# An AdaLN, recurrence and mixture-of-experts block: order of batch 3's steps, expert order from two batches, batch 0 in halves, the condition by a product

## The chip, the cores and the metric

One Trainium2 chip, one core. The time is device microseconds of the whole program; the figure of the kernel before is the median of three runs.

## The reference, cut to what matters

Four batches of 256 tokens with 256 channels, all in float32. `side` gives both keys and values.

```python
def wkv(r, k, v, w, u, time_emb):               # two directions of a decayed sum over the tokens
    tf = sigmoid(sum(time_emb))                 # one number a batch, from the condition
    decay = exp(-exp(w)) * (0.5 + 0.5 * tf)
    ek = exp(min(k, 30)); ekv = ek * v
    nf, df = forward scans;  nb, db = reverse scans
    num = nf + nb - ekv + exp(u + k) * v;  den = df + db - ek + exp(u + k)
    return sigmoid(r) * num / max(den, 1e-8) * (0.8 + 0.2 * tf)

def recurrence(x, W_in, b_in, W_gate, b_gate, lam):
    alpha = exp(-8 * softplus(lam) * sigmoid(x @ W_gate + b_gate))
    h = scan(alpha, sqrt(1 - alpha**2 + 1e-6) * sigmoid(x @ W_in + b_in) * x)
    return h

def ffn(x, w_router, wg, wu, wd, sg, su, sd):   # 8 experts, top 2, and 2 shared ones; 640 hidden
    scores = sigmoid(x @ w_router.T)            # the two best, weights made to sum to 1
    return routed experts (SwiGLU) + shared experts (SwiGLU)

x = x + recurrence(wkv(x, side, side, w1, u1, cond), ...)
x = x + ffn(wkv(x, side, side, w2, u2, cond), ...)
```

The router weighs each token's logits; an expert computes only the tokens that chose it.

## The kernel before

Activations are channel-major: a tile holds 128 channels by 2 x 256 columns (two halves of the channels, the tokens of one batch). A 512-column operation covers a batch.

**Start.** `par` (small vectors), `cond` (spread to all 128 partitions by the DMA), batch 0's `x` and `wio` are issued on ACT's queue, the `side` tiles, batch 1, `wr` and the two shared experts (`shared`) on SP's. PE runs warm-up products of `ident` meanwhile (L355 plain, L358 in four tiled quarters; WARM sets how many).

**A batch's front** (`front(b)`). `half_tanh` (xc), `exps` (L447 to L461), `sums` (reverse scans L479, forward scans L547 on DVE; for batch 0 the parts are added on PE by products with `ident`, L509; elsewhere on DVE, L534 and L536, or by an adding DMA, L523), `most` (L563), `quotient` (Ln and Exp on ACT, L579 and L580; L581, L582, L584 on DVE), `gates` (L601, products with `wio` L612, tanh L620, square root L649), `recurrence` (L656, scans L661, sum into x L667, tanh L668, product L670, giving `xt`). `fill` (L518) puts products of `ident` on PE where it would stand idle during batch 0. Then `token_rows`: transposes of `xt` (L748), router products (L753), `scores` (L759), copies into token rows (L762).

**Routing.** `route` turns scores into ranks, `chosen`, `upto` (a running count by tile of 128 tokens) and `comb` (L778 to L805). It runs once for batches 0 to 2 and once for batch 3. `places` counts with two products (`counted`: L892 with `ones` and `upto`, L893 with `before` and `chosen`) and gives each token its row in an expert's region; `scatter` (L1110, POOL) sends token rows there, and eight `blank` DMAs (L1123, ACT's queue) put empty rows behind each region's last. In the call for batches 0 to 2, a third product (L896) counts what was chosen so far, and `line_up` ranks the experts by it, busiest first, into `order_eid`; `first_weights` then loads the weights of the first four experts (`quad`, three DMAs of 640 KB each, L1202). `divide` (L1033 to L1107), after batch 3, deals the remaining tiles of 128 tokens to slots; their weights go to a `ring`.

**Shared experts** (`shared_units(b)`). Two experts of five units each: four products of 256 columns into one of four PSUM banks (L836), SiLU (L842, ACT), product (L844, DVE), and two down products a unit (L821), up to three units later. Base rows: transposes of x (L859), copies (L863), sum with the shared result (L865), output DMA (L879, SP).

**Experts.** The list of slots and groups runs after everything above: transposes of gathered rows (L1189), gate and up products (L1212), SiLU and product (L1217, L1218), down products (L1225), weighting (L1232), scatter-add into the output (L1241, POOL). LAST dummy products (L1501) on PE end it; a branch (L1503) for more tiles follows, which isn't taken with these inputs.

**What sets the order.** All before the experts is recorded as steps in the class `Plan`: engine, length, what it reads and writes, a rank (smaller goes first), and `late`, the time after a step's end until another engine may take its result for done. `Plan.run` goes through time: at each point the engine whose next step can start earliest takes the ready step of lowest rank. NUDGE adds to the ranks of single steps. The steps are then emitted in that order, and every engine executes its own list strictly in it. The lengths and `late` are only the planner's figures; on the chip each instruction waits for what it truly needs.

Of the kernel before, what the change touches and what calls it, by code (L numbers as in the profile page):

```python
# [8 lines left out]
F32 = mybir.dt.float32  # L9
# [9 lines left out]
P = 128  # L19
# [39 lines left out]
ACTS, DEPTH, WARM, KEEP, FILL, LAST = 6, 3, 12, 6, 4, 7  # L59
# [27 lines left out]
    ("divide", "dve", "blank_row"): -6,  # L87
    ("exps", 0, "act", "ek"): -5,
    ("exps", 0, "act", "own"): -6,
    ("exps", 0, "dve", "own"): 1,  # L90
    ("exps", 1, "dve", "ek"): -6,
    ("exps", 2, "dve", "ek"): 14,
    ("exps", 2, "dve", "own"): 9,
    ("exps", 3, "dve", "ek"): 6,
    ("exps", 3, "dve", "own"): 5,
    ("factors", "dve", "decay1"): 14,
    ("gates", 1, "act", "gate"): 5,
    ("gates", 1, "act", "xb"): -5,
    ("gates", 2, "pe", "one"): 6,
    ("gates", 3, "act", "gate"): 5,  # L100
    ("gates", 3, "act", "xb"): -5,
    ("gates", 3, "dve", "xc"): 10,
    ("line_up", "dve", "order_at"): 11,
    ("loads", "act", "xr"): 2,
    ("most", 3, 2, "act", "fwd"): 5,
    ("places", 0, "pe", "one"): 9,
    ("quotient", 1, 2, "act", "inv"): 16,
    ("quotient", 1, 2, "dve", "fwd"): 20,
    ("recurrence", 0, "dve", "xt"): 12,
    ("recurrence", 3, "dve", "xb"): 7,  # L110
    ("route", 0, "dve", "comb"): 1,
    ("route", 0, "dve", "upto"): 5,
    ("route", 3, "dve", "comb"): -5,
    ("rows", 0, "dve", "scores"): 24,
    ("rows", 2, "dve", "scores"): 23,
    ("rows", 2, "pe", "one"): 5,
    ("rows", 3, "pe", "one"): 7,
    ("shared", 0, "act", "act"): 37,
    ("shared", 0, "pe", "acc"): -4,
    ("shared", 0, "pe", "bank"): -6,  # L120
    ("shared", 1, "pe", "bank"): -1,
    ("shared", 1, "pe", "one"): -10,
    ("shared", 2, "pe", "acc"): 1,
    ("sums", 0, 1, "dve", "fwd"): 1,
    ("sums", 0, 1, "dve", "rev"): 1,
    ("sums", 0, 2, "pe", "bank"): -5,
    ("sums", 1, 1, "dve", "rev"): -13,
    ("sums", 1, 2, "dve", "fwd"): 4,
    ("sums", 1, 2, "dve", "own"): 3,
    ("sums", 1, 2, "dve", "rev"): 5,  # L130
    ("sums", 2, 1, "dve", "fwd"): 1,
    ("sums", 2, 2, "dve", "fwd"): -3,
    ("sums", 2, 2, "dve", "rev"): -3,
    ("sums", 3, 2, "dve", "fwd"): -15,
    ("sums", 3, 2, "dve", "own"): 5,
    ("sums", 3, 2, "dve", "rev"): 4,
# [102 lines left out]
def adaln_attn_ffn(ctx: ExitStack, tc, xT, sideT, cond, par, wio, wr, wall, out):  # L239
# [17 lines left out]
    cond_sb = fixed("cond_sb", B, TD)  # L257
    nc.scalar.dma_start(cond_sb, cond.partition_broadcast(P))
# [20 lines left out]
    load_batch(0, nc.scalar)  # L279
    nc.scalar.dma_start(wio_sb, wio)  # L280
# [7 lines left out]
    nc.scalar.preload_act_table_set(EXP)  # L288
    ident = fixed("ident", P)
# [64 lines left out]
    for k in range(WARM):  # L354
        nc.tensor.matmul(banks[k % BANKS][:, 0, 0:P], ident, ident, start=True, stop=True)  # L355
    for k in range(2 * WARM):
        q = 32 * (k % 4)
        nc.tensor.matmul(  # L358
            banks[k // 8][q : q + 32].rearrange("p g t -> p (g t)")[:, 0:P], ident[:, 0:32], ident,
            start=True, stop=True, tile_position=(0, q),  # L360
        )
    acc = [psum.tile([P, 2 * C], F32, name=f"acc{j}")[:, 0:C] for j in range(TB)]
    ones_ps = [psum.tile([P, 2, T], F32, name=f"one{k}") for k in range(2)]
# [4 lines left out]
    def halves(name, *rest):  # L368
        return [(name, *rest, h) for h in range(2)]

# [9 lines left out]
    def pe(cols, emit, reads=(), writes=(), rank=0, **kw):  # L380
        return step("pe", 1.625 * cols + 16, emit, reads, writes, rank, late=205, **kw)
# [8 lines left out]
    given(("side", 0), 4400)  # L390
    given("cond", 4600)
    given(("x", 0), 6000)
    given("wio", 8000)
    given(("side", 1), 8500)
    given(("x", 1), 9000)
# [4 lines left out]
    given(("x", 2), 23000)  # L400

    def factors():

        plan.part = ("factors",)
        dve(250, lambda: nc.vector.tensor_reduce(tf, cond_sb, AX.X, ALU.add), ["cond"], ["tf"], 11)
# [109 lines left out]
    def fill(after, times, writes=()):  # L515

        for k in range(times):
            pe(P, lambda: nc.tensor.matmul(acc[1][:, 0:P], ident, ident, start=True, stop=True), (), writes, 99, after=[after])  # L518
# [46 lines left out]
    def quotient(b, n):  # L565
# [9 lines left out]
        if (b, n) in BY_PE:  # L575
# [7 lines left out]
        dve(  # L583
            512, lambda: nc.vector.scalar_tensor_tensor(f[:, NC:, :], num, out_tf[:, b : b + 1], y, ALU.mult, ALU.mult),  # L584
            nkeys + yk + ["out_tf"], ns, r,
        )
        return f[:, NC:, :], ns

    def half_tanh(b):
        plan.part = ("half_tanh", b)  # L590
        act(
            512, lambda: nc.scalar.activation(xc, xs[b], AF.Tanh, scale=0.5), [("x", b % 3)], ["xc"], 10 * b + 19,
# [3 lines left out]
    def gates(b, q, qkeys):  # L596
# [4 lines left out]
        dve(512, lambda: nc.vector.scalar_tensor_tensor(xc, xc, 1.0, q, ALU.add, ALU.mult), ["xc"] + qkeys, ["xc"], r)  # L601
        for which, dst, name in ((1, gate, "gate"), (0, xb, "xb")):
# [6 lines left out]
            for m, (key, pio) in enumerate(to):  # L609
                for k in range(NC):  # L610
# [5 lines left out]
                        ["xc", "wio"], [key], 0,  # L616
# [9 lines left out]
        dve(512, lambda: nc.vector.scalar_tensor_tensor(xb, xb, 1.0, xc, ALU.add, ALU.mult), xbs + ["xc"], xbs, r + 1)  # L626
# [22 lines left out]
        act(512, lambda: nc.scalar.activation(gate, gate, AF.Sqrt, bias=eps, scale=-1.0), gs, gs, r, tables=(SQRT,), hold=(name, True))  # L649
# [959 lines left out]
```

## Time and profile before

| | |
|---|---|
| median of three runs | 297.46 us (297.28 to 297.73) |
| the profiled execution | 296.47 us |
| its span | 294.8 us |
| mean granted clock of PE | 0.985 of full speed |
| PE, DVE, ACT, POOL busy | 95%, 59%, 43%, 21% of the span |
| bytes moved by DMA | 51.68 MB |
| first scan on DVE | 8.23 us |
| token rows of batches 0, 1, 2, 3 begin on PE | 32.07, 63.90, 94.76, 124.55 us |
| first transpose of the expert stretch | 162.59 us |

A row of the timeline is: start in us, length in us, engine, line, operation, tile written <- tiles read, shapes, count; in brackets the idle time before and what ended it. Rows of the same line in a row are drawn together. A float32 product of 256 columns shows as two records, one of 128 columns also as two. A row of windows gives, per engine, busy time and number of instructions, then PE's granted clock, the share of the DMA engines in use and GB/s. "SPq" and "ACTq" are DMA issues on that queue.

### The profile page before, as it was taken

What the parts mean: (1) busy time and instruction counts of PE and PEld (TensorE: products, weight loads), DVE (VectorE), ACT (ScalarE), POOL (GpSimd) and SP (SyncE); (2) the same over time, 40 slices, a digit from 0 to 9 for tenths busy, and PEclk for the clock granted to TensorE, in tenths of its full rate; (3) what the DMA queues carried; (4) which work ended last, traced back from release to release, by engine and by line L of the source; (5) the groups of instructions that cost most, each with busy time, mean ns of one, the idle gap of its engine ahead of it and who ended that gap; (6) DMA issues with size and microseconds to landing.
All of it is one profiled execution on the core that took longest, in us unless ns stands there. A gap on an engine that the chain in (4) does not pass through costs nothing. (4 is left out here: it accounts for less than half of the span.)

```text
span 294.8 us, 5521 instructions
## 1 busy us (share of the span) xinstructions
PE 281.2 (95%) x1945; PEld 243.5 (83%) x1945; DVE 173.6 (59%) x493; ACT 127.6 (43%) x253; POOL 61.4 (21%) x102
## 2 busy tenths in 40 slices
PE   7999999999999999995999999999999999999990
PEld 7889888888888888874888768999868997698990
DVE  3999999999999987944532443223443225334220
ACT  5768879967395869750111221122121112112200
POOL 8820000000100011771300002210142222242421
PEclk9999999999999999997899999999999999999998
DMA  4962030002300040279988999999847798322211
GB/s 141 425 275 91 3 71 0 2 0 71 71 2 1 0 86 23 95 263 419 299 280 279 395 413 409 374 395 394 294 88 255 229 382 302 57 27 31 23 22 22
DMA packets 19665, 51.68 MB, mean 175 GB/s; under 512 B 2736, under 2 KB 11824, under 8 KB 19376
## 3 DMA queue, kind: packets, MB, share of 16 engines
q1 hardware_dynamic: 13216, 42.46, 37.9%
q0 software_dynamic: 3792, 6.06, 11.0%
q10 hardware_dynamic: 2624, 2.74, 2.8%
q8 instruction: 17, 0.28, 0.4%
q14 instruction: 16, 0.13, 0.1%
HBM read 54.43 MB, written 7.05 MB: 209 GB/s over the span
## 5 line engine op out<-in xcount | busy, mean ns | idle before, releaser
L836 PE MATMUL bank<-xt,shared 128*128 128x256 f32 x320 | 75.0, 389 | 0.0
L836 PEld LDWEIGHTS bank<-xt,shared 128*128 128x128 f32 x320 | 62.2, 196 | 8.6
L1212 PE MATMUL bank<-side,late 128*128 128x128 f32 x400 | 47.7, 276 | 0.0
L1212 PEld LDWEIGHTS bank<-side,late 128*128 128x128 f32 x400 | 46.3, 192 | 1.3 <-issue 1.0
L1218 DVE TENSOR_TENSOR act<-bank,act 128x256 f32<-128x256 f32 (+1 forms) x42 | 15.9, 380 | 47.1 <-ACT act L1217 43.5
L1241 POOL DMA_INDIRECT outT<-ys,to x14 | 21.6, 1546 | 101.4 <-DMA xr<-rows 37.4
L1217 ACT ACTIVATE act<-bank 128x256 f32<-128x256 f32 (+1 forms) x42 | 14.6, 349 | 54.1 <-PE bank L1212 50.2
L821 PE MATMUL acc<-shared,act 128*128 128x256 f32 x160 | 37.9, 381 | 0.1
L821 PEld LDWEIGHTS acc<-shared,act 128*128 128x128 f32 x160 | 30.1, 190 | 4.5 <-DVE act L844 0.5
L221 ACT ACT_TABLE_LOAD x24 | 30.8, 1283 | 0.4
L842 ACT ACTIVATE act<-bank 128x256 f32<-128x256 f32 x40 | 13.8, 383 | 31.4 <-PE bank L836 16.7
L844 DVE TENSOR_TENSOR act<-bank,act 128x256 f32<-128x256 f32 x40 | 15.6, 417 | 15.1 <-ACT act L842 14.1
L1225 PE MATMUL acc<-late,act 128*128 128x256 f32 x100 | 23.4, 381 | 0.0
L1232 DVE TENSOR_SCALAR ys<-acc,w 128x256 f32<-128x256 f32 (+1 forms) x18 | 8.5, 472 | 23.2 <-PE acc L1225 16.3
L523 POOL DMA_DIRECT2D late<-late x3 | 2.9, 952 | 87.2 <-DVE late L536 37.7
L547 DVE TENSOR_TENSOR_SCAN late<-decay,late 128x256 f32<-128x256 f32 x32 | 20.8, 674 | 0.0
L1225 PEld LDWEIGHTS acc<-late,act 128*128 128x128 f32 x100 | 18.2, 190 | 3.1 <-issue 0.5
L1110 POOL DMA_INDIRECT rows<-xtok,where x16 | 16.6, 1036 | 20.0 <-DVE at L919 10.0
L1192 ACT COPY side<-one 128x256 f32<-128x256 f32 x17 | 6.2, 373 | 33.5 <-PE one L1189 31.1
L479 DVE TENSOR_TENSOR_SCAN late<-late,decay 128x255 f32<-128x255 f32 x32 | 20.2, 669 | 0.0
L1212 PEld LDWEIGHTS bank<-side,quad 128*128 128x128 f32 x120 | 13.9, 192 | 1.1 <-issue 0.5
L1212 PE MATMUL bank<-side,quad 128*128 128x128 f32 x120 | 14.5, 277 | 0.2 <-ACT side L1192 0.2
(256 smaller groups left out, 396.4 us busy)
## 6 DMA issues: line engine op xcount, KB each, us to landing
late<-in_wall SPq DMA_DIRECT2D x33, 640.0 KB
quad<-in_wall SPq DMA_DIRECT2D x27, 640.0 KB
shared<-in_wall SPq DMA_DIRECT2D x9, 640.0 KB
shared<-in_wall SPq DMA_DIRECT2D x2, 1920.0 KB
late<-late POOLq DMA_DIRECT2D x3, 512.0 KB
xr<-rows SPq DMA_DIRECT2D x10, 136.0 KB
rows<-empty ACTq DMA_DIRECT2D x8, 136.0 KB
side<-in_sideT SPq DMA_DIRECT2D x4, 256.0 KB
```

The lines of the kernel that those rows point to most:

```text
L221: order.append((max(free.get(engine, 0), 0), len(order), lambda t=table: load_table(t)))
L479: 0, lambda h=h, c=c: nc.vector.tensor_tensor_scan(r[:, h, 0 : T - 1][:, ::-1], src[:, h, 1:T][:, ::-1], dec[:, c, b : b + 1].to_broadcast ...
L547: 0, lambda: nc.vector.tensor_tensor_scan(f[:, h, :], dec[:, c, b : b + 1].to_broadcast([P, T]), src[:, h, :], 0.0, ALU.mult, ALU.add),
L821: 256, lambda j=j: nc.tensor.matmul(acc[j], acts[a][:, bass.ts(j, P)], shared[s][:, GU + i * C : GU + (i + 1) * C], start=((s, i) == (0, 0 ...
L836: 256, lambda ps=ps, gu=gu, g=g, c=c, i=i: nc.tensor.matmul(ps[:, g, :], gu[:, g, c, bass.ts(i, P)], xt[k][:, c, :], start=(c == 0), stop= ...
L844: 256, lambda ps=ps, av=av: nc.vector.tensor_tensor(av, ps[:, 1, :], av, ALU.mult),
L1110: i = nc.gpsimd.indirect_dma_start(out=rows[:, :], out_offset=bass.IndirectOffsetOnAxis(ap=where[:, k, t : t + 1].bitcast(U32), axis=0), i ...
L1212: nc.tensor.matmul(ps[:, g, i, :], gu[:, g, k, bass.ts(i0 + i, P)], self.xg[:, k, :], start=(k == 0), stop=(k == NC - 1),)
L1217: nc.scalar.activation(hid[:, 0:n, :], ps[:, 0, 0:n, :], AF.Silu)
L1218: nc.vector.tensor_tensor(hid[:, 0:n, :], ps[:, 1, 0:n, :], hid[:, 0:n, :], ALU.mult)
L1225: nc.tensor.matmul(self.py, self.acts[i], self.weights[:, GU + i * C : GU + (i + 1) * C], start=(i == 0), stop=(i == NI - 1),)
L1241: nc.gpsimd.indirect_dma_start(out=out[:, :], out_offset=bass.IndirectOffsetOnAxis(ap=to.bitcast(U32), axis=0), in_=ys, in_offset=None, bo ...
```

## The change

- **Order of batch 3.** A step on PE may be given its own `late`. The products of the first two units of the first shared expert of batch 3 get 4200 ns instead of 205. With the ranks in NUDGE (a new table throughout) and scatter's `late` of 4000, the emitted order becomes: on DVE all of `route` directly behind batch 3's scores, `places` next, then L844 of unit 2, unit 0 and unit 1; on ACT SiLU of unit 2, unit 0, one blank-row DMA, unit 1, seven blank-row DMAs, then the other units; on PE behind the token rows two products of unit 0, four transposes (L859), two more, four of unit 1, two of unit 2, the counting pair, and the rest.
- **Expert order from batches 0 and 1** (NGUESS). A new `guess()` takes the scores (logits) of the first two batches before `route`, holds them at SAME = 16.7, takes off a thousandth of the expert's number, marks the two largest of each token, counts with four products of `ones`, and calls `line_up`. L896 and the call in `places` fall away. `first_weights` is split: the first two experts' weights are issued on SP after the tanh of batches 1 and 2, the other two after that of batch 3.
- **Batch 0's last steps in halves.** `x`, `xc` and `xt` carry keys by half, and for batch 0 the last step of the first quotient, the first of the gates, the square root, L656, L667, L668 and L670 are emitted as two 256-column operations. Token-row transposes and shared products wait for the half they read.
- **The condition by a product.** `cond` is loaded as one row of 1 KB on SP and spread by a product of a row of ones into PSUM (`cond_all`), which DVE reduces. In the emitted order that product is the first on PE. All first loads but `par` go on SP: side 0, cond, x 0, wio, side 1, x 1, wr, shared.
- WARM 12 to 4 (plain products 2 x 4, tiled 3 x 4, instead of 12 and 24), FILL 4 to 3, LAST 7 to 14. The fill products write a part of PSUM that nothing else uses.

```diff
-ACTS, DEPTH, WARM, KEEP, FILL, LAST = 6, 3, 12, 6, 4, 7
+ACTS, DEPTH, WARM, KEEP, FILL, LAST = 6, 3, 4, 6, 3, 14
+NGUESS = 2
+SAME = 16.7
 NUDGE = {
...
-    cond_sb = fixed("cond_sb", B, TD)
-    nc.scalar.dma_start(cond_sb, cond.partition_broadcast(P))
+    cond_sb = fixed("cond_sb", B * TD)
...
-    load_batch(0, nc.scalar)
-    nc.scalar.dma_start(wio_sb, wio)
+    load_side(0)
+    nc.sync.dma_start(cond_sb[0:1, :], cond.rearrange("b d -> (b d)").unsqueeze(0))
+    load_x(0, nc.sync)
+    nc.sync.dma_start(wio_sb, wio)
...
-    for k in range(WARM):
+    cond_all = ones_ps[1][:, 0, 0 : B * TD]
+    for k in range(2 * WARM):
         nc.tensor.matmul(banks[k % BANKS][:, 0, 0:P], ident, ident, start=True, stop=True)
-    for k in range(2 * WARM):
+        if k == WARM - 1:
+            nc.tensor.matmul(cond_all, ones[0:1, :], cond_sb[0:1, :], start=True, stop=True)
+    for k in range(3 * WARM):
...
+    def parts(b):
+        return [(c, slice(c, c + 1)) for c in range(NC)] if b == 0 else [(None, slice(0, NC))]
...
-        dve(512, lambda: nc.vector.scalar_tensor_tensor(xc, xc, 1.0, q, ALU.add, ALU.mult), ["xc"] + qkeys, ["xc"], r)
+        for c, at in parts(b):
+            dve(
+                size(c), lambda at=at: nc.vector.scalar_tensor_tensor(xc[:, at], xc[:, at], 1.0, q[:, at], ALU.add, ALU.mult),
+                some(halves("xc"), c) + some(qkeys, c), some(halves("xc"), c), r,
+            )
...
-                            [("xt", k), ("shared", s)], [("bank", q)], 10 + b,
+                            [("xt", k, c), ("shared", s)], [("bank", q)], 10 + b,
+                            late=4200 if b == B - 1 and s == 0 and i < 2 else 205,
...
+    def guess():
+        plan.part = ("guess",)
+        n = NGUESS * TB
+        top, picks = (cond_sb[:, at : at + n * E].rearrange("p (t e) -> p t e", e=E) for at in (0, n * E))
+        keys = [("scores", b, j) for b in range(NGUESS) for j in range(TB)]
+        r = 10 * NGUESS + 9
+        full = [P, n, E]
+        dve(
+            n * E, lambda: nc.vector.scalar_tensor_tensor(
+                picks, scores[:, 0:n, :], SAME, little.to_broadcast(full), ALU.min, ALU.subtract
+            ), keys, ["picks"], r,
+        )
+        for t in range(n):
+            dve(8, lambda t=t: nc.vector.max(out=top[:, t, :], in_=picks[:, t, :]), ["picks"], ["top"], r)
+        dve(n * E, lambda: nc.vector.tensor_tensor(picks, picks, top[:, :, 1:2].to_broadcast(full), ALU.is_ge), ["top", "picks"], ["picks"], r)
+        o = turn_of("one", 2)
+        so_far = ones_ps[o].rearrange("p a t -> p (a t)")[:, 0:E]
+        for t in range(n):
+            pe(32, lambda t=t: nc.tensor.matmul(so_far, ones, picks[:, t, :], start=(t == 0), stop=(t == n - 1)), ["picks"], [("one", o)], 9)
+        line_up(so_far, [("one", o)], r + 5)
...
-        if last < B:
-            line_up(so_far, pk, r - 2, begun_beta[last])
...
-                    [("spread", t, k)], 10 * last + 20, length=1280, late=5200 if last == B else 2500,
+                    [("spread", t, k)], 10 * last + 20, length=1280, late=4000 if last == B else 2500,
...
-    def first_weights(behind_):
-        plan.part = ("weights",)
+    def first_weights(j, behind_):
+        plan.part = ("weights", j)
         gone = [("ek", 0, 0), ("ek", 0, 1), *halves("own", 1, 0), *halves("own", 2, 0), ("inv", 1)]
-        for j in range(4):
-            writes = [("quad", j), *(gone if j == 3 else [])]
-            dma("sp", lambda j=j: groups[0].load_weights(j), ["order_eid"], writes, 1 + j, late=12000, after=[behind_])
+        writes = [("quad", j), *(gone if j == 3 else [])]
+        dma("sp", lambda: groups[0].load_weights(j), ["order_eid"], writes, 1 + j, late=7000, after=[behind_])
...
+        if b + 1 == NGUESS:
+            guess()
+        if b > 1:
+            first_weights(b - 2, begun[b - 1])
...
+    for j in (2, 3):
+        first_weights(j, begun[B - 1])
     shared_units(B - 1)
```

## The prediction

> **What bounds the kernel now.** I read the page's busy shares and 40 slices first.
>
> ```profile
> PE 281.2 (95%) x1945; PEld 243.5 (83%) x1945; DVE 173.6 (59%) x493; ACT 127.6 (43%) x253; POOL 61.4 (21%) x102
> PE   7999999999999999995999999999999999999990
> DVE  3999999999999987944532443223443225334220
> PEclk9999999999999999997899999999999999999998
> DMA  4962030002300040279988999999847798322211
> ```
>
> PE carries the span. One slice of it is open (the 19th, a 5), and there the granted clock dips. DVE is full in slices 2 to 14 (7 to 103 us): until then DVE and PE are both tight. Next the stretch around the open slice, in windows of 10 us (columns: length, then PE, PEld, DVE, ACT, POOL busy, clock, DMA share, GB/s), and PE's timeline there:
>
> ```profile
> 120.00:130.00 10.00, 10.00 (x56) 8.72 (x54) 6.04 (x17) 7.78 (x13) 7.87 (x8) 1.00 0.46 153
> 130.00:140.00 10.00, 6.27 (x24) 5.13 (x23) 5.38 (x35) 0.66 (x2) 3.40 (x4) 0.79 1.02 403
> 140.00:150.00 10.00, 10.00 (x42) 8.58 (x41) 6.75 (x43) 2.18 (x6) 2.92 (x3) 0.87 0.94 315
> ```
>
> ```profile
> 125.81 1.11 PE L821 MATMUL acc<-shared,act 128*128 128x256 f32 x4
> ...
> 128.49 3.62 PE L836 MATMUL bank<-xt,shared 128*128 128x256 f32 x16
> 135.83 0.62 PE L892 MATMUL one<-upto,ones 128*128 128x24 f32 x2 [3.73 <-DVE upto L796]
> ...
> 136.71 2.05 PE L836 MATMUL bank<-xt,shared 128*128 128x256 f32 x4
> ...
> 153.96 8.80 PE L821 MATMUL acc<-shared,act 128*128 128x256 f32 x40
> 162.59 0.60 PE L1189 MATMUL one<-ident,xr 128*128 128x128 f32 x4
> ```
>
> After the last token rows PE has 6 us of other work, then stands 3.73 us for `upto`, then runs at half clock (0.50 in 2-us windows from 136 to 142, 0.84 in 142 to 144). What it lost: from 153.96 to 162.59 forty records take 8.63 us, 0.216 each. From 125.81 to 162.59 there are 130 such records (28.1 us), eight transposes (0.88) and the counting pair (0.4): 29.4 us of work in 36.8 us. The gap costs **7.4 us**: 3.7 of waiting, 3.7 of half clock. Behind 163 us PE's timeline shows no gap, so time saved here reaches the end.
>
> Why `upto` is late is in DVE's and ACT's timelines:
>
> ```profile
> 131.92 0.17 DVE L800 SCALAR_TENSOR_TENSOR comb<-ranks,scores 128x16 f32<-128x16 f32 x1
> 134.71 0.42 DVE L844 TENSOR_TENSOR act<-bank,act 128x256 f32<-128x256 f32 x1 [2.61 <-ACT act L842]
> 135.05 0.17 DVE L793 TENSOR_SCALAR chosen<-ranks 128x16 f32<-128x16 f32 x1
> ...
> 135.62 0.16 DVE L796 TENSOR_TENSOR upto<-upto,chosen 128x8 f32<-128x8 f32 x1
> ```
>
> ```profile
> 134.29 0.66 ACT L842 ACTIVATE act<-bank 128x256 f32<-128x256 f32 x2 [4.37 <-remote]
> ```
>
> DVE runs in order, and an L844 of batch 3's first unit stands ahead of `chosen` and `upto`. It waits for ACT's L842, which waits 4.37 us for "remote", though PE ended that unit's four matmuls by about 130.3 (128.49 plus eight records of 0.216). Its result is 4 us late; the profile doesn't say why. The weights' burst (DMA share 1.02) and POOL's scatters run at that time.
>
> **The change, part by part**, against the profiled 296.47 us (span 294.8 and 1.67 around it; 0.99 below the median of the runs).
>
> *Batch 3's order.* The route steps now follow the scores on DVE with no L844 or L865 between, `places` next, the products last. When does `upto` come? By the rows of before: scores' end at 126.16, table load and exp, L781's end at 128.58, five compare steps 1.49 (130.43 to 131.92), `chosen` and two `upto` steps 0.73: 130.8, or 4.96 us behind the token rows' end on PE (125.81). PE's cover up to the counting pair is now ten matmuls of 0.432 and four transposes: 4.76 us instead of 6.06. Wait there: 0.2 us. Later waits: PE's fifth unit needs the bank of the first one read, whose results may again be late: 0 to 1.8 us, and 0.7 is taken as POOL's scatters still run then but less is loaded. ACT now issues seven blank-row DMAs in a row; pairs take 1.24 to 1.90 us in before, so 4 to 7 us without a SiLU against four banks: 0 to 1.1, taken 0.5. Loads of rows for the experts, pushed back by this: 0 to 1, taken 0.3. Sum 1.7 of new waits (0.5 to 4.0), all under 3.73, so no half clock. Gain 7.4 − 1.7 = **5.7** (3.4 to 6.9).
>
> *The Trainium skill* ("TensorE: Matmul & The Clock Gate", Part 1) says that one window of about 3.4 us without work halves the clock and one full of work restores it. The row of 3.73 us idle with 0.50 behind it agrees; by the page a new wait of 3.4 would already cost as much again, by the row 3.73.
>
> *Expert order from batches 0 and 1.* DVE gets six small steps (min, four max, compare) of 0.16 to 0.28: 1.1 us. They fall into 64 to 118 us, and the ordering steps of `line_up` move ahead with them; slices 15 and 16 of DVE (8 and 7) have 3 us open. PE gets four matmuls of 8 columns, nearest row L753 (0.51 for 4 records, two matmuls), 0.9 us, and loses one of L896, 0.2: **+0.7** (0.3 to 0.9), PE having no gap there. Two of the four first weight loads (three DMAs of 640 KB each) now leave SP earlier, into slices with DMA digits of 0 to 7, and the burst at 130 is halved. On SP they stand ahead of batch 1's output DMA, which waits behind them for `order_eid`; its tile is next written by batch 3's base at about 148 us, so that wait has some 30 us of cover; without it batch 3's copies would wait for the DMA. The ordering only says which experts lead; the number of full tiles stays, so the stretch behind 163 us is taken unchanged (0).
>
> *Start.* The condition comes as one row and is spread by a PE product, which stands first on PE's queue. Before, PE warmed up from 1.79 on and DVE had `cond_sb` at 5.97:
>
> ```profile
> 1.79 4.98 PE L355 MATMUL bank<-ident 128*128 128x128 f32 x24 [1.79 <-POOL ident masks.py:199]
> 25.89 5.52 PE L518 MATMUL acc<-ident 128*128 128x128 f32 x48
> 5.97 0.42 DVE L405 TENSOR_REDUCE tf<-cond_sb 128x4 f32<-128x256 f32 x1 [0.60 <-DMA cond_sb<-in_cond]
> ```
>
> The first 24 records take 207 ns each, the same form later 115: cold until about 6. No row shows a 1 KB load; par, the smallest, was issued at 0.81 and used at 2.49, so 1.7 us, and the row, second on SP, lands at 3 to 4, taken 3.7. Without the broadcast, batch 0's side can land before 5.44, where ACT took it up (bounds 2.5 to 5.4, taken 4.5 as its bytes stay): first scan about 7.3 instead of 8.23. But PE starts 1.9 us later with 8 and 12 warm-ups for 24 records and 48 tiled ones. From the first scan pair's end, 8.5, the first bank needs ten 256-column records and three fills (six records): 10 × 0.216 + 6 × 0.115 = 2.9 warm (11.4), 10 × 0.43 (twice 0.216) + 6 × 0.207 = 5.5 cold (14.0). Taken 13.4, nearer cold, since the row of the start is cold for 4.3 us from the first record. L563 read it at 12.22 before, and DVE's L581 came 3.42 later: now 16.8 instead of 15.64. From there to the end of `xt` DVE has 14.6 us of work (512 columns or a scan 0.60, a half 0.36), where before took 16.4: `xt` of batch 0 ends at 31.4 instead of 32.02. Two scans (1.2) that lay before it are now owed before batch 1's, where L748 waited 0.2 in before: token rows of batch 1 come **+0.6** later (−1.0 with a warm PE, +1.4 with a colder one). The halves cost DVE 0.08 a pair, in the 14.6.
>
> By the same page PE stays at half rate until 3.4 us of unbroken work lie behind it; its rule speaks against cutting the warm-ups, and would put the bank at 14.0 and token rows at +1.2. No run of before shows a late start.
>
> *Priced at nothing:* LAST from 7 to 14, as PE ends at about 289 and the last scatter at 287.07 to 294: 1.7 us more of dummies lie beside it; without that cover 1.7. FILL and WARM counts, beyond the above, run while PE waits for DVE. First loads all on SP: ACT has 2.3 us of issues less in front of its table load at 3.08.
>
> Sum: −5.7 + 0.6 + 0.7 = −4.4, so 292.1 profiled and **293.0** at the median's level.
>
> **Rivals.**
> 1. *The gap comes back* (slower). If lateness of 4 us belongs to whatever PE finishes first in this stretch, and not to the units' banks, it falls on the token rows themselves. The point: `upto` more than 8.5 us behind them (cover 4.76 and a wait of 3.73); then 7.4 is lost again, ACT's blanks cost 0.5 more, start and guess 1.3: 298.3 profiled, 299.2. For it: the cover shrank by 1.3 us. Against: in before the scores came 0.2 us behind PE, not late.
> 2. *Half the gain.* The late banks stop PE at its fifth unit in several waits of 1 to 3 us, no half clock: 4.2 lost, gain 3.2, with a start of +1.2: −1.3, or 296.1 (294.5 to 297.5). For it: "remote" took 4.37 us once, four units of PE work last 6.9, and seven blanks come on top. Against: half the burst is gone.
> 3. *No lateness any more.* If the burst made it, halving it ends it; waits 0.5 and a warm start: −6.9 − 0.5 + 0.7 = −6.7, or 290.8 (289.5 to 291.3).
> 4. *DVE becomes the bound to 118 us.* If the open slices don't take the 1.1 us and the moved ordering steps, up to 2 us come on top of the main case: 295.
>
> **How the numbers follow.** Main case 0.50 (291.3 to 294.5, from waits of 0.5 to 3 and the start's two ends, not all at once), rival 1 0.18, rival 2 0.14, rival 3 0.12, rival 4 0.06. A measurement here tells about 0.2%, 0.6 us, from no change: faster is below 296.9, slower above 298.1. Faster: 0.50 + 0.12 + 0.06 + two thirds of rival 2 = 0.77, less 0.02 for what I don't see; same 0.06; slower 0.19. The range leaves out the low edge of rival 3 and most of rival 1: 290.0 to 297.8; the main case alone is 291.3 to 294.5.
>
> **What would show it.** Right: no idle above 1.8 us ahead of PE's L892 equivalent, clock 1.00 in every 2-us window of 130 to 146, about 31 us from the last token rows to the first expert transpose, DVE's `upto` 5 us behind the scores. The start: first scan near 7.3, `xt` of batch 0 near 31.4, token rows of batch 1 near 64.5. Wrong: a wait over 3.7 us on the counting pair or a fifth unit, half clock anywhere behind 10 us, or PE idle at every token rows (DVE bound).

## The result, and the profile after

The changed kernel takes 300.46 us (median of eight runs, 299.31 to 302.94) where the kernel before, beside it, takes 297.3 (eight runs, 295.34 to 299.18): a ratio of 1.0119, 95% interval 1.0078 to 1.0159. It is slower, by 1.2%. Its profiled execution is 299.31 us with a span of 297.5, 2.7 more than before.

The page of the changed kernel, three rows of its 40 slices:

```profile
PE   4999899989999999994899999999999999999994
PEclk9999999999999999999599999999999999999999
DMA  6952030002349197032497897899729599312121
```

The open slice of PE is still there: the 19th, as before, now with part of the 20th (the 4 and the 8), and the granted clock dips there again (the 5). The DMA row shows that the weights' burst is gone from it: 2 and 4 where before had 9s. The windows across it (columns as before), and PE's timeline:

```profile
130.00:140.00 10.00, 7.12 (x36) 5.70 (x34) 2.85 (x14) 2.90 (x5) 7.11 (x8) 1.00 0.28 104
140.00:150.00 10.00, 7.68 (x23) 6.35 (x24) 8.49 (x58) 1.04 (x3) 3.95 (x4) 0.66 0.49 147
```

```profile
127.61 0.38 PE L789 MATMUL one<-ident,xt 128*128 128x128 f32 x2
...
133.99 0.40 PE L934 MATMUL one<-upto,ones 128*128 128x24 f32 x2 [0.17 <-DVE upto L837]
134.23 0.38 PE L935 MATMUL one<-chosen,before 128*128 128x24 f32 x2
134.45 2.84 PE L877 MATMUL bank<-xt,shared 128*128 128x256 f32 x12
142.32 8.13 PE L877 MATMUL bank<-xt,shared 128*128 128x256 f32 x24 [5.03 <-DVE act L886]
...
166.75 0.60 PE L1250 MATMUL one<-ident,xr 128*128 128x128 f32 x4
```

The counting pair (L934, L935; L892 and L893 before) waits 0.17 us instead of 3.73. But PE then stands 5.03 us for the bank of batch 3's fifth unit, and runs at half clock from 142 to 147 us (0.50 in both 2-us windows from 142 to 146, 0.55 from 146 to 148). What it waits for is the same lateness as before, one consumer further on; ACT, DVE and POOL show it:

```profile
138.26 0.98 POOL L1171 DMA_INDIRECT rows<-xtok,where  x1 [0.30 <-issue]
140.37 0.17 DVE L975 TENSOR_TENSOR place<-one,heads 128x16 f32<-128x16 f32 x1 [6.15 <-remote]
141.09 0.66 ACT L884 ACTIVATE act<-bank 128x256 f32<-128x256 f32 x2 [8.16 <-remote]
```

The counting pair ends at 134.61 (134.23 and 0.38), and DVE, idle, starts on its result at 140.37: 5.8 us late. ACT's first SiLU starts at 141.09 on products that ended by 136. The last of POOL's twelve scatters of batches 0 to 2 ends at 139.24, just before. (In before: the twelfth ended at 133.03, ACT took the late result at 134.29.)

Where the 2.7 us of span went, by the starts on PE in the two profiles:

| stretch | before | changed | difference |
|---|---|---|---|
| start to batch 0's token rows | 32.07 | 32.20 | +0.13 |
| to batch 1's | 31.83 | 33.57 | +1.74 |
| to batch 2's | 30.86 | 32.02 | +1.16 |
| to batch 3's | 29.79 | 29.82 | +0.03 |
| to the first expert transpose | 38.04 | 39.14 | +1.10 |
| to the last scatter-add | 124.48 | 124.48 | 0.00 |
| to the end of the span | 7.73 | 6.27 | −1.46 |

The front loses 3.06 us, the gap, which was to shrink, grows by 1.1, and the tail gives 1.46 back. The second stretch in windows, before and changed:

```profile
32.07:63.90 31.83, 31.70 (x155) 27.69 (x156) 31.21 (x58) 26.84 (x48) 1.11 (x1) 1.00 0.09 18
```

```profile
32.20:65.77 33.57, 32.29 (x157) 27.84 (x157) 32.68 (x61) 27.98 (x49) 1.11 (x1) 1.00 0.09 16
```

DVE is full in both (98% and 97%), and has 1.47 us more to do: the timeline counts 23 scans there instead of 20. They were left over from before batch 0's `xt`. The third stretch holds the four count products (0.81 us on PE at 81.06), which stand in a PE stream without gaps; the other 0.35 us of its 1.16 was not traced.

### The profile page after: what moved, and what is told of

Its sections match the earlier page's. It is cut to its first block, busy times and chain, and to the rows that moved or that the text cites. A ratio compares the mean times of both kernels' runs of the same rounds, so it can differ in the third digit from the quotient of the medians.

```text
span 297.5 us, 5488 instructions
## 1 busy us (share of the span) xinstructions
PE 281.0 (94%) x1919; PEld 241.5 (81%) x1919; DVE 176.0 (59%) x504; ACT 126.9 (43%) x254; POOL 61.0 (21%) x103
## 4 chain that ended last, share of the span: by engine, by line
PE 73%; ACT 13%; DVE 8%; another core or an unknown queue 3%; issue 1%; DMA 1%; SPq 0%; DVEq 0%
PE bank L1273 21%; PE bank L877 14%; PE acc L1286 10%; PE acc L862 7%; PE bank L1351 5%; ACT L216 4%; PE one L636 3%; PE bank L526 3%; PE acc L1368 2%; PE one L1250 1%; DVE act L886 1%; ACT late L596 1%; PE bank L359 1%; PE bank L1562 1%
## 5 line engine op out<-in xcount | busy, mean ns | idle before, releaser
L1302 POOL DMA_INDIRECT outT<-ys,to x14 | 21.8, 1554 | 93.0 <-DVE ys L1293 39.5
L862 PE MATMUL acc<-shared,act 128*128 128x256 f32 x160 | 37.1, 382 | 1.1 <-DVE act L886 1.0
L886 DVE TENSOR_TENSOR act<-bank,act 128x256 f32<-128x256 f32 x40 | 15.5, 417 | 13.5 <-ACT act L884 13.3
L1253 ACT COPY side<-one 128x256 f32<-128x256 f32 x17 | 6.2, 373 | 31.5 <-PE one L1250 31.4
```

What stands on the lines that cost most here:

```text
L862: 256, lambda j=j: nc.tensor.matmul(acc[j], acts[a][:, bass.ts(j, P)], shared[s][:, GU + i * C : GU + (i + 1) * C], start=((s, i) == (0, 0 ...
L886: 256, lambda ps=ps, av=av: nc.vector.tensor_tensor(av, ps[:, 1, :], av, ALU.mult),
L1302: nc.gpsimd.indirect_dma_start(out=out[:, :], out_offset=bass.IndirectOffsetOnAxis(ap=to.bitcast(U32), axis=0), in_=ys, in_offset=None, bo ...
```

## Experiments

All ratios are against the kernel before, run beside it on the same chip. Chips turned out to matter, so the experiments are told chip by chip, in the order in which they ran. "Gap stretch" is the time from batch 3's token rows to the first expert transpose, of which 30.6 us is PE work (the 29.4 of the prediction and the token rows).

### First chip: what makes the signals late, and what the start costs

A result of PE is called late here when its consumer, idle, starts some microseconds behind the end of PE's record. Theory A: a run of scatters on POOL holds back PE's completion signals. Theory B: what PE ends first behind batch 3's token rows is late by itself.

**e1, scatters behind.** POOL issues the twelve scatters of batches 0 to 2 behind the four of batch 3.

```diff
+    def scatter_late(t, k):
+        if t < (B - 1) * TB:
+            kept_back.append((t, k))
+            return
...
-                    lambda t=t, k=k: scatter_row(t, k),
+                    lambda t=t, k=k: scatter_late(t, k),
```

> The changed kernel with POOL's twelve scatters of batches 0 to 2 issued behind the four of batch 3 instead of ahead of them; every other engine's order is as it was. Theory A (a run of scatters on POOL holds back PE's completion signals; in both traces they come late from some 9 us into the run until 1.2 us behind its end): from 130 to 141 us nothing is late, the SiLU of batch 3's first unit starts within 0.1 us of the modelled end of its products instead of 5.5 us later, PE does not wait 5.03 us for a bank and the clock stays 1.00 there; lateness comes later, some 9 us into the run that now begins at about 136. The scatters end at about 157 instead of 147, so expert rows come some 5 us later, and the time is -1 to +4 us. Theory B (what PE ends first behind batch 3's token rows is late of itself): the same wait of 5 us at the same place, and the time +3 to +6 us.

304.2 us, ratio 1.0276 (1.0212 to 1.034). No signal was late anywhere, the clock did not dip at 140; but ACT, with the expert-row loads on its queue ahead of the last SiLUs, stood 17.5 us for the late scatters, and PE 8.38 us.

**e2, scatters spread.** Six small POOL operations ahead of each of the twelve.

```diff
+        if t < (B - 1) * TB:
+            for _ in range(6):
+                nc.gpsimd.tensor_scalar(ser, ser, 1.0, None, ALU.mult)
+        scatter_row(t, k)
```

> The changed kernel with six small POOL operations ahead of each of the twelve scatters, which spreads them from a pitch of 1.3 us to some 2.6; every other engine's order is as it was. Theory A, if it is the density of scatters that holds PE's signals back: no late signal, no wait of 5.03 us for a bank, no half clock, so -8 us at the first expert transpose less up to 2 for scatters that end later: time -8 to -5 us. Theory A, if it is any scatter under way: lateness of the same size or longer, time 0 to +5. Theory B: a wait of 5 us as before, time 0.

311.17 us, ratio 1.0507 (1.0437 to 1.0576). The pitch became 3.3 us, nothing was late, and PE stood 16.62 us for the same row loads. Where scatters end decides when the rows can be loaded; that price I had put at 0 to 2 us.

**e3, old start.** Loads, the spread of `cond` by DMA, and warm-ups of before.

```diff
+    nc.scalar.dma_start(cond_sb.rearrange("p (b d) -> p b d", b=B), cond.partition_broadcast(P))
...
-    load_side(0)
-    nc.sync.dma_start(cond_sb[0:1, :], cond.rearrange("b d -> (b d)").unsqueeze(0))
-    load_x(0, nc.sync)
-    nc.sync.dma_start(wio_sb, wio)
+    load_batch(0, nc.scalar)
+    nc.scalar.dma_start(wio_sb, wio)
...
-    for k in range(2 * WARM):
+    for k in range(12):
...
-    for k in range(3 * WARM):
+    for k in range(24):
...
```

> The changed kernel with the first loads, the spread of the condition by the DMA and the 12 and 24 warm-up products of the kernel before; DVE's and ACT's order as in the changed kernel. If the late start and cold clock of PE cost the 1.87 us by which batch 1's token rows came later (65.77 against 63.90), these come at 63.5 to 64.5 and the time falls by 1.3 to 2.2 us, unless the wait behind it swallows it. If the order of the scans costs it, token rows stay at 65.2 to 66 and the time within 0.6 us.

294.04 us, ratio 0.9935 (0.9902 to 0.9968). Token rows of batch 1 at 65.44: of the 1.87 us, the start is 0.33. The rest is not the start; the count of scans above points to their order. The interval from batch 0's rows to batch 1's is 33.5 us in every kernel with the changed front, whatever its start, and 31.8 in every profile of before.

**e4, warm-ups first.** 12 plain products, then the condition's, then 24 tiled ones.

> The changed kernel with 12 plain warm-up products ahead of the condition's product and 24 tiled ones behind it, instead of the product first and 8 and 12. PE is then at full clock from about 6.1 us, the product runs at about 6.5 and DVE's reduction some 1.3 us later than 5.82; first scan at 8.3 to 9.0, the first bank's sum at 12.2 to 12.8 instead of 13.5. If the cold clock is what costs, token rows of batch 1 come 0.7 to 1.3 us earlier and the time falls by as much; if it is the order of the scans, they stay.

295.16 us, ratio 0.9982 (0.9947 to 1.0018). Token rows of batch 1 at 66.44, none earlier. `tf`'s reduction came at 8.40, and DVE's first scan at 10.26, both 2.58 us later than in the change. So this run does not tell what a warm clock alone is worth.

In e3 and e4 nothing was late either, though POOL's queue was untouched: neither theory had that. The gap stretch was 34.3 and 35.0 us.

### Second chip: the same again

Theory C: the lateness belongs to the chip.

> The changed kernel once more, beside the others of this call on one chip. In the first four experiments no completion signal of PE was late, though two of them changed nothing but POOL's queue and two nothing but the start. Theory C (the lateness belongs to the chip or the execution, and not to the program): on a chip where it is absent the first expert transpose comes 34 to 36 us behind the last token rows, as in those runs, instead of 39.1, with the clock at 1.00 throughout, and the time is within 1 us of the old-start variant of this call and 1 us or less from the kernel before. Theory A (POOL's run of scatters): late again by 4 to 6 us with a half clock behind it, 3 us slower than before.

300.73 us, ratio 1.0104 (1.0048 to 1.016): late as in the first profile, gap stretch 39.5, and this wait for a bank:

```profile
143.82 7.00 PE L877 MATMUL bank<-xt,shared 128*128 128x256 f32 x24 [5.38 <-DVE act L886]
```

> The kernel before once more, for its profile on this chip. Theory C: if nothing is late on this chip, L842 starts within 0.1 us of the end of its products, the counting pair waits under 1 us and the gap of 7.4 us is not there; if it is late, it is late in the kernels of this call alike. Theory A: late by 4 us as in its first profile, whatever the chip.

Late too: the pair waits 5.58 us, the gap stretch is 39.4 (one execution of 299.62 us).

> The changed kernel with the twelve scatters behind the four, as before. If the unchanged change is late on this chip and this is not, scatters cause the lateness (theory A); if both are late, the chip does (theory C); if neither, nothing of this is told apart. The wait for the rows (8.4 us at the last SiLUs) comes in any case.

This one tells most, though it is one execution (305.85 us). PE, POOL and ACT of the kernel with the scatters behind, on this chip:

```profile
143.93 2.32 PE L862 MATMUL acc<-shared,act 128*128 128x256 f32 x10
156.88 3.68 PE L877 MATMUL bank<-xt,shared 128*128 128x256 f32 x8 [10.62 <-issue]
```

```profile
156.84 0.98 POOL L1171 DMA_INDIRECT rows<-xtok,where  x1 [0.31 <-issue]
```

```profile
136.37 0.66 ACT L884 ACTIVATE act<-bank 128x256 f32<-128x256 f32 x2 [2.44 <-PE bank L877]
...
155.98 0.39 ACT L884 ACTIVATE act<-bank 128x256 f32<-128x256 f32 x1 [16.55 <-remote]
```

At 130 to 143 us, where the change is late on this very chip, nothing is: the first SiLU starts at 136.37, at once behind its products. The run of sixteen scatters starts at 137.14; the first result that is late is one of 144.5, and the last late one arrives at 160.3, 2.4 us behind the end of the last scatter (157.82). The lateness moved with the scatters. So A and C hold together: in the runs on some chips, a run of scatters makes PE's results late, from 7 us into it here (13 us in the first profile of before, whose first late result is that of 130.3) until 1 to 3 us after its end.

> The changed kernel with the old start, as before. Token rows of batch 1 at 65.4 again. Theory C: late if the change is late on this chip, and then within 1 us of it; not late if that isn't, and 0.3 to 1 us faster than it. If it is not late while the change is late, the start has to do with the lateness, and 4 to 6 us lie between them.

299.28 us, ratio 1.0066 (1.0039 to 1.0094). Late as the others on this chip (bank wait 5.46); 1.45 us under the change, from a start that ran 2.2 us ahead in the profiles (batch 0's rows at 31.16 against 33.33); on the first chip e3's 31.92 was only 0.3 ahead of the first profile's 32.20.

### Third chip: does more cover at the bank help?

Five down products of batch 2 that stood behind the seventh unit go ahead of the fifth, on PE alone.

```diff
+        for n in of(("shared", 2), "acc"):
+            start, seq, emit = order[at[n]]
+            if start > fifth:
+                order[at[n]] = (fifth - 1, seq, emit)
```

> The changed kernel with the five remaining down products of batch 2 (ten records, 2.16 us) put on PE ahead of batch 3's fifth unit, where PE stood 5.03 us for a bank; all else in its order. If PE's wait there is set by late signals of the first units (theory A with C, a chip on which they are late): the wait falls to 2.9 us, which is under the 3.7 us behind which the clock halved, so the half clock (2.7 us lost) goes too, and the time falls by 4 to 5 us against the change. On a chip where nothing is late: 0 to -0.7 us. Rival (the clock halves in any case, or the wait moves on with the work): -2.2 us or less.

> The same with the old start of the third experiment. The start was worth 0.3 us of the token rows of batch 1 on one chip and 2.2 on another, so 0.3 to 2.2 us less than the kernel with the down products ahead alone; on a chip with late signals that is 4 to 7 us less than the change, 1 to 3 us less than the kernel before. Rival: no sum, the wait for expert rows behind it takes the gain back.

This chip has no late signals. e9: 296.15, ratio 1.0038 (1.0005 to 1.0071); e10: 293.93, ratio 0.9951 (0.9921 to 0.9981), so faster than before here.

> The kernel before, for its profile on this chip. If signals are late here: a gap of 7 to 9 us behind batch 3's token rows, as in both profiles so far. If they are not late: L842 of the first unit at once behind its products, a wait of 1 us or less at the counting pair, and a gap under 3 us, so that the change has little to take away.

The kernel before where nothing is late (one execution, 297.05 us), PE and ACT:

```profile
131.65 0.40 PE L892 MATMUL one<-upto,ones 128*128 128x24 f32 x2
...
155.36 5.41 PE L821 MATMUL acc<-shared,act 128*128 128x256 f32 x16 [3.57 <-DVE act L844]
160.61 0.60 PE L1189 MATMUL one<-ident,xr 128*128 128x128 f32 x4
```

```profile
154.47 0.38 ACT L842 ACTIVATE act<-bank 128x256 f32<-128x256 f32 x1 [7.36 <-issue]
```

No wait at the pair, as expected, but 3.57 us near the end, with a half clock behind it (0.61 and 0.54 in the windows from 155 to 159): ACT stood with the row loads of the experts at the head of its queue, ahead of SiLUs whose inputs were there. The gap stretch is 36.4 us and not under 33.6: there is a second wait behind the first, and the first hid it.

> The changed kernel with POOL's twelve scatters at a pitch of 3.3 us instead of 1.3, as in the second experiment, where that chip showed no lateness in any kernel. On a chip with late signals: if the density of scatters makes them late, none is late here; if the number of scatters under way or their time does, they are late again from the sixth to eighth scatter (some 25 us behind the first) or from 9 us on, until the last. The wait of 16 us for the rows comes in any case, so the time says nothing.

Nothing late (the chip has none), 311.11 us in one execution.

### Fourth chip: the single step

The rest asks what in the change would have been worth having, in the kernel before.

```diff
+        for n in of(("shared", 3), "act", "dve"):
+            start, seq, emit = order[at[n]]
+            if start <= route:
+                order[at[n]] = (route + 1, seq, emit)
```

`route` is the place of DVE's last route step; the L844 of batch 3's first unit, which stood ahead of it, goes behind it.

> The kernel before with one step moved on DVE: the product L844 of batch 3's first unit goes behind the last route step instead of ahead of chosen and upto. Nothing else moves. If the gap of the kernel before is DVE's order, as the prediction has it, then on a chip with late signals the counting pair waits under 0.5 us, PE has work up to some 136 us, the late results (about 134.3) free the banks before that, no half clock: the gap of 7.4 us falls to 0.5 to 2 and the time by 5 to 7 us. Rival (the late signals catch PE at the fifth unit, as they did in the change): a wait of 1 to 4 us there and a gain of 0 to 4. On a chip without late signals: 0 within 0.3 us, since the pair doesn't wait there.

294.67 us, ratio 0.9953 (0.9919 to 0.9988), on a chip with late signals:

```profile
133.21 0.40 PE L907 MATMUL one<-upto,ones 128*128 128x24 f32 x2 [0.70 <-issue]
...
136.10 0.66 PE L874 MATMUL one<-ident,x 128*128 128x128 f32 x4 [1.31 <-DVE counts L1048]
...
158.18 0.85 PE L1204 MATMUL one<-ident,xr 128*128 128x128 f32 x4
```

Two waits of 0.70 and 1.31, no half clock, gap stretch 33.2 instead of 38 to 39: 4.8 us under the first profile of before, but only 1.3 off the median, where 5 to 7 were forecast. The profiled execution is the fastest of the twelve (292.18 us, mean granted clock 1.000); the others took 292.74 to 295.51 at 0.986 to 0.997. How much of the gain they lost to a half clock, and how much to scatter-adds that wait for one another's landing (below), is not shown. It is the only kernel here that beat the kernel before on a chip with late signals.

On ACT, the eight row loads behind the last SiLU as well:

> The same, and on ACT the eight loads of expert rows go behind the last SiLU of batch 3 instead of among the last four. If row loads that wait for scatters and blank rows to land hold up the SiLUs (3.57 us of PE's wait and 1.7 of half clock in the kernel before on a chip without late signals): on such a chip 3 to 5 us less than before; on a chip with late signals 0 to 1 less than the kernel with DVE's order alone. Rival (PE then waits for the rows themselves at the first expert transpose): a gain of 0 to 1, with PE idle ahead of L1189.

296.57 us, ratio 1.003 (0.9995 to 1.0064): the rival. PE has no wait for SiLUs, and then stands 1.43 and 0.81 us for the rows at the first transposes; its profile also has a half clock from 135.0 and from 162.3 us, for 3.4 us each. No single wait ahead of the first was long:

```profile
132.39 0.40 PE L912 MATMUL one<-upto,ones 128*128 128x24 f32 x2 [0.69 <-DVE upto L816]
...
135.25 1.12 PE L879 MATMUL one<-ident,x 128*128 128x128 f32 x4 [1.28 <-DVE counts L1053]
```

In the 3.4 us up to 135.0 PE worked for 1.7 us in all.

> The changed kernel once more. On a chip without late signals: first expert transpose 34 to 36 us behind the last token rows, token rows of batches 1, 2, 3 late against the kernel before by 2, 3 and 3 us as everywhere, and a time of -0.5 to +1 us against before. On a chip with late signals: 39 us and +3 us, as twice before.

299.71 us, ratio 1.0104 (1.004 to 1.0169), late, gap stretch 40.2.

> The changed kernel with the five down products ahead and the old start, as before (293.93 against 295.39 on a chip without late signals). On a chip with late signals: PE waits 2.9 us at the fifth unit instead of 5.03, the clock stays at 1.00, and the time is 4 to 7 us under the change's 3 us loss, so 1 to 4 under the kernel before. Rival: the clock halves all the same, and it is 0 to 2 over the kernel before.

299.1 us, ratio 1.0114 (1.0056 to 1.0172): the rival again.

```profile
141.80 7.13 PE L890 MATMUL bank<-xt,shared 128*128 128x256 f32 x24 [3.40 <-DVE act L899]
151.06 5.45 PE L890 MATMUL bank<-xt,shared 128*128 128x256 f32 x24 [1.69 <-DVE act L899]
```

The bank wait fell as it should, but 3.40 us was enough for the clock (0.58 and 0.57 in the windows from 142 to 146), and the seven blank-row issues then held the SiLUs for another 1.69.

### Fifth chip

> The changed kernel with POOL's twelve scatters at a pitch of 3.3 us instead of 1.3. On a chip with late signals: if density makes them late, the SiLU of batch 3's first unit starts within 0.1 us of its products' end (about 136) and nothing is late up to 165; if the mere presence of scatters does, signals are late by 4 us or more from some point behind the sixth to eighth scatter (141 to 152) until the last (165). The wait for rows of 16 us comes in any case. On a chip without: as twice before, nothing late.

> The changed kernel once more, with a profile. On a chip without late signals: 34 to 36 us from batch 3's token rows to the first expert transpose, clock 1.00, span 292 to 295. On one with late signals: 39 to 40 us and a span of 297 to 299, as before.

No late signals here. e17 (311.35 us) repeats e12, so whether spacing the scatters cures the lateness was not answered. e18 is the change without lateness, 296.67 us where before took 295.56 in one execution each:

```profile
134.76 0.40 PE L934 MATMUL one<-upto,ones 128*128 128x24 f32 x2 [0.15 <-DVE upto L837]
...
147.53 5.45 PE L877 MATMUL bank<-xt,shared 128*128 128x256 f32 x24 [1.03 <-DVE act L886]
...
162.28 1.99 PE L862 MATMUL acc<-shared,act 128*128 128x256 f32 x8 [1.71 <-DVE act L886]
164.11 0.60 PE L1250 MATMUL one<-ident,xr 128*128 128x128 f32 x4
```

The gap stretch is 35.7, with 0.39 and 1.03 us lost to blank rows and 0.35 and 1.71 to row loads on ACT's queue. Against the 36.4 of before without lateness (e11) that is a gain of 0.7, less than the front costs: without late signals the change has little to take away.

## Why the prediction was wrong

**Right.** The cause of the old gap: DVE's order put `chosen` and `upto` behind a late SiLU. e13 moves that one step and the pair's wait falls from 3.73 us to 0.70. `upto`'s new time: forecast 4.96 us behind the token rows' end (the rows it was added up from give 4.99) and a wait of 0.2; measured 5.12 and 0.17. The start: the row of `cond` at 3.73 (3.7), first scan 7.68 (7.3), the first bank read at 13.53 (13.4), DVE's first quotient step 16.95 (16.8). The expert stretch: 124.48 us in both, as said; LAST and FILL were not tried alone.

**The step that failed** is the sentence "all under 3.73, so no half clock", and in it the bank wait of the fifth unit, priced at 0 to 1.8 us and taken as 0.7. It was 5.03, with 2.7 of half clock behind it (5.47 us of PE work at half rate): 7.7 where 0.7 stood, so the gap of 7.4 became 8.5 and not 1.7. The condition was wrong as well as the size: the clock halved behind a wait of 3.40 us in e16, and behind two of 0.69 and 1.28 us in e14. I had sized the lateness as the 4 us of one row, and reasoned that half the burst meant less of it. The first profile of the change, late at a DMA share of 0.28, and e7 show that the burst was not its source. The scatters were: the lateness lasts until they end, and the change starts them later (at 123.64 against 116.99), and later relative to batch 3's token rows too: 4.0 us ahead of them (127.61) instead of 7.6 (124.55). The same lateness therefore reached 12.8 us past the token rows instead of 9.7 (140.37 and 134.29 less the two starts). Rival 1 named the mechanism, but at the counting pair; the condition it needed, late token rows, was not met, and the gap came back at a consumer that I had priced as small; that its 299.2 us lies near the result is luck. Rival 2 had the right consumer, the fifth unit, but with waits of 1 to 3 us and no half clock. Rival 3 fails on both counts: the burst was not the source, and where nothing is late the change is no faster than before (e18).

**The front** was mis-sized: +0.6 forecast for token rows of batch 1, +1.87 measured. Three scans were owed, not two, and `xt` of batch 0 did not come earlier to pay for them: it ended at 32.48 and not at 31.4, since DVE took 15.5 us to it from the first quotient step and not 14.6. Its rows were at 32.2 to 33.3 in the profiles of the change, 31.7 to 32.7 in those of before and its variants, 31.2 to 32.0 with the old start. Part of that spread goes with PE's rate at the start, which rises at another time in each execution of the same program: the 24 tiled warm-ups took 0.86 us in the first profile of the change (rows at 32.20), 1.10 in e15 (32.68) and 1.51 in e5 (33.33). The first pair of profiles, with 0.13 between them, was a lucky one. The guess's stretch cost 1.16 where 0.7 was forecast.

**The half clock.** The Trainium skill ("TensorE: Matmul & The Clock Gate", Part 1) gave a window of about 3.4 us; I set the row's 3.73 beside it as the bound. Waits of 3.40 (e16) and 3.57 us (e11) both halved the clock, for 3.4 us each, so the page's length agrees, and the row was only one instance above it. The longer waits of the change halved it for 3.4 us (e5) or 6.8 (its first profile), that is for one or two such windows. But e14 differs from the page's rule of a window without work: its clock halved with PE at work for half of the 3.4 us before. e13, with waits of 0.70 and 1.31 us, kept its clock. So short waits close together can do it too, and a limit on each single wait is no safe rule; what share of work keeps the clock up was not measured.

**Unforeseen in the change's favour**: the tail. In the first pair of profiles the 1.46 lies behind the last scatter-add, where one part of it landed late in before (at 292.36 us, the others by 290.92): 7.73 us to the end of the span, 6.1 to 6.5 in every other profile. More often it lies ahead of it. In all fifteen profiles of kernels with the changed order of experts the last scatter-add starts 124.5 to 124.6 us behind the first transpose. In those of the kernel before and its two variants it is 124.5, 126.1, 127.3, 127.3 and 128.6, since scatter-adds wait for the one before to land (the last one of e11 for 4.65 us). Whether the order of experts or the fourteen dummies do that was not tried.

**What stays open.** Why scatters make PE's results late is not shown, nor whether the results or only their signals are late: the ends of PE's records are modelled. Nor is it shown why on some chips only (late in the first pair of profiles and on the second and fourth chip, not on the first, third and fifth): each chip was measured at one time only, so what differs may be the time and not the chip. Spacing the scatters was only tried where nothing is late.

## What to carry to other kernels

When a result is late for a reason that the profile does not name, an order that moves one consumer out of its way only moves the wait to the next: list every consumer (here the pair, then the banks, then ACT's DMA issues) and price each with the whole lateness, to where its source ends, before counting a gain. Change the one step that the trace accuses alone first: here one DVE product moved behind the route steps (0.995 of before) beat, on the same chip, a change of five parts (1.010), which costs 3 us in the tight front. And where a stretch is full on DVE, count the instructions that are owed to the next stretch, not only those that leave this one.

## What the runs showed of the hardware

- PE's results can be taken late by 4 to over 10 us, while its records run on at 0.216 us each: in the changed kernel's profile results of 134.6 and about 135.6 were taken at 140.4 and 141.1, and in e7, with the scatters moved, those of 144.5 to 146.3 at 156 to 160. Signals between ACT and DVE in that time were not late: in e7 DVE took ACT's SiLU of 156.37 at 156.40.
- It happens in the runs on some chips and not in those on others, with the same program: gap stretches of the change of 39.1 us in the first profile, 39.5 and 40.2 on the second and fourth chip, 35.7 on the fifth. The mean granted clock of every execution points the same way: 0.986 to 0.994 in all 30 where the changed front met late signals with its scatters in place (first result, e5, e8, e15, e16), 0.996 or more in 42 of 45 where nothing was late (e3, e4, e9, e10, e18).
- The clock of PE halves for 3.4 us or a multiple (6.8 in the first profile of the change, 10.2 behind e1's wait of 8.38 us). In e14 it did so behind waits of 0.69 and 1.28 us.
- An engine's queue is held by a DMA issue at its head: seven blank-row issues in a row took ACT 5.8 to 6.8 us, and row loads that wait for data kept ACT from its next SiLU for 17.5 us (e1) or 25.8 (e2).
